# Attention's small work dealt out anew among ACT, DVE and POOL in a fused attention and mixture-of-experts kernel

## The chip, the cores and the metric

The kernel runs on one core of one Trainium2 chip. The metric is the device time of one execution in microseconds (us). The core has five engines with queues of their own, each of which works strictly in its queue's order: TensorE (PE in the profile, its weight loads PEld), VectorE (DVE), ScalarE (ACT), GpSimd (POOL) and SyncE (SP), which here only issues transfers. Engines wait for each other by semaphores.

## The reference

Sixteen batches of 128 tokens of width 512 go through two blocks, all in fp32:

```python
x = x + xattn(layernorm(x), ctx, ctx)     # 32 query heads, 8 key heads of width 16; keys = values = ctx
x = x + ffn(layernorm(x))                 # gate over 32 experts, top 8 in 4 of 8 groups, plus a shared expert

def layernorm(x, eps=1e-5):
    m = mean(x); v = var(x)
    return (x - m) / sqrt(v + eps)
```

In the attention each key head of 16 columns serves four query heads; scores are divided by 4 (the root of the head's width), go through a softmax and weight the values. In the second block each token's normalised row is multiplied with the gate's weights; the gate's best eight experts and the shared expert compute `(silu(x @ w1.T) * (x @ w3.T)) @ w2.T`, and the experts' results are added with the gate's weights.

## The kernel before

**The whole.** `attention_small()` (L271) computes both normalisations, the attention and the gate's logits. `experts()` (L1011) then routes the tokens (`route()`, L1088), computes the shared expert, gathers each expert's tokens from a table `rows` in memory (L1411), multiplies them with the expert's weights (L1483, L1537) and adds them to the output (L1509). The change touches attention alone.

**The order** of PE, DVE, ACT and POOL inside attention is the program's order, written out by hand (`manual_schedule`, L182). The tile framework adds the semaphore waits that the data and the buffers need. Instructions that read or write one and the same PSUM tile are kept in order as well.

**Steps.** An item is a batch b and a parity i: half of the key heads of that batch. There are 32 items, `items[n] = (n // 2, n % 2)`, and step n of the loop at L615 does, in this order:

1. the functions listed for the head of step n (`head`, L616);
2. `scores(n)` (L449): four row-packed matmuls into two PSUM tiles `sc` (two buffers in all), and on ACT two exps `p` of 128x1024 (L464);
3. `values(n - 1)` (L467): four matmuls into `oT` (one buffer), copied to `oTs` by DVE (L479);
4. in some steps `gate_parts` (L528: four matmuls and a copy on ACT, L540);
5. `transposes(*sets)` (L414): PE turns up to two sets of 128x512 into halves of one PSUM tile `x` (one buffer). The sets are `queries(n // 2 + 1)` (L439) in even steps, `added(n - 2)` (L499), and `turn_of(b)` (L506) from step 13 on, mostly in odd steps. When all are turned, each set's own function uses its half: for queries a copy to `qT` (L445, on DVE), for an attention output `add` (L485: on DVE the reciprocal `ri`, L488, and the product `at`, L490; on POOL the addition to `x`, L497), for a gate row a copy to `xnT` (L508, on ACT);
6. in some steps `gate_sums` (L542: two small matmuls and a copy to `logits` on DVE, L549);
7. the functions listed for the tail of step n (`tail`, L638).

**What the heads and tails hold** (L566 to L611):

- `layernorm_stats(b, mv)` (L89): on DVE `bn_stats` (L91) and `bn_aggr` (L92) of one batch. The first normalisation's run at steps 0 to 15, two in some of them. The second normalisation's need both halves of a batch added on POOL; batch b's stand at the tail of step 2b + 4, those of batch 13 at the head of step 30.
- `layernorm_rstd` (L94): 1/sqrt(v + eps) by a guess and three Newton rounds, 14 small instructions on POOL or 11 on DVE, for a group of batches at once. The first normalisation has groups of 1 and 3 on DVE and of 4, 4 and 4 on POOL (steps 3, 8 and 16), the second four groups of 3 and one of 2 on POOL (steps 9, 15, 21, 27 and 30) and one of 2 on DVE behind the loop.
- `rows_of(b)` (L390): on DVE the normalised queries `xq` of a batch.
- `keys(k)` (L342): for four batches at once, the transposed context times a mask of odd or even heads, two instructions of 128x512 into `kz`. The first quarter's are on ACT (L346), the other three quarters' on POOL (L348) at the heads of steps 4, 9 and 17. `values_of(k)` (L354) copies the values `va` of four batches: ACT for the first quarter, POOL for the others.
- `gate_rows(b)` (L215): the second normalisation's row `xn` (L217), on POOL for batches 0 to 11 and on DVE for 12 to 15, and one store of 256 KB to `rows` from SP (L220). Rows 9, 10 and 11 stand at the heads of steps 28, 29 and 30.
- `key_lengths(k)` (L364): ACT squares a quarter's context (L366), DVE sums it (L371), at steps 17 to 20; the longest is found at step 21.

**Before the loop** ACT holds, in this order, the two keys of the first quarter (L346) and `values_of(0)` (L355, which waits for the load of `cn`); DVE holds the first batch's statistic, its Newton rounds, its queries and the first copy to `qT`. **Behind the loop** (L643 to L683) come the last outputs, the last gate rows and their logits, with the first matmuls of the shared expert as filler; `both` (L656) is one PSUM tile whose halves take turned gate rows and the last output.

Of the kernel before, what the change touches and what calls it, by code (L numbers as in the profile page):

```python
# [9 lines left out]
F32 = mybir.dt.float32  # L10
# [36 lines left out]
def tile_xattn_moe(  # L47
# [40 lines left out]

    def layernorm_stats(b, mv):  # L89
        st = xnp.tile([P, 6], F32, tag="st", name="st")  # L90
        nc.vector.bn_stats(st, xs[b])  # L91
        nc.vector.bn_aggr(mv[:, b, :], st)  # L92

    def layernorm_rstd(mv, rstd, eng):  # L94

        n = mv.shape[1]
        ve = xnp.tile([P, B], F32, tag="ve", name="ve")[:, 0:n]
        eng.tensor_scalar(ve, mv[:, :, 1], EPS, None, ALU.add)
        r = xnp.tile([P, B], I32, tag="r", name="r")[:, 0:n]
        eng.tensor_scalar(  # L100
            r, ve.bitcast(I32), -0.5, float(0x5F3759DF), ALU.mult, ALU.add
        )
        r = r.bitcast(F32)
        h = xnp.tile([P, B], F32, tag="h", name="h")[:, 0:n]
        for i in range(3):
            to = rstd if i == 2 else r
            if eng is nc.vector:
                eng.scalar_tensor_tensor(h, r, -0.5, r, ALU.mult, ALU.mult)
                eng.tensor_tensor(h, h, ve, ALU.mult)
                eng.scalar_tensor_tensor(to, h, 1.5, r, ALU.add, ALU.mult)  # L110
            else:
                eng.tensor_tensor(h, r, r, ALU.mult)
                eng.tensor_tensor(h, h, ve, ALU.mult)
                eng.tensor_scalar(h, h, -0.5, 1.5, ALU.mult, ALU.add)
                eng.tensor_tensor(to, h, r, ALU.mult)

    def normalized_T(b, mv, rstd, dst, ps_tr):

        xn = xnp.tile([P, D], F32, tag="xn", name="xn")
        nc.vector.tensor_scalar(  # L120
            xn, xs[b], mv[:, b, 0:1], rstd[:, b : b + 1], ALU.subtract, ALU.mult
        )
        tr = ps_tr.tile([P, ND, P], F32, tag="tr", name="tr")
        for k in range(ND):
            nc.tensor.transpose(tr[:, k, :], xn[:, ts(k, P)], ident)
        nc.scalar.copy(dst, tr)
        return xn
# [4 lines left out]
    sap = ctx.enter_context(tc.tile_pool(name="sap", bufs=1))  # L132
    mv1 = const.tile([P, B, 2], F32, name="mv1")
    rstd1 = const.tile([P, B], F32, name="rstd1")
    mv2 = const.tile([P, B, 2], F32, name="mv2")
    rstd2 = const.tile([P, B], F32, name="rstd2")
    logits = const.tile([P, NT, E], F32, name="logits")
# [17 lines left out]
    more = const.tile([1, 1], I32, name="more")  # L155

    def first_rstd(first, n, eng=nc.vector):
        bs = slice(first, first + n)
        layernorm_rstd(mv1[:, bs, :], rstd1[:, bs], eng)

# [47 lines left out]

    def second_rstd(first, n, eng=nc.vector):
        bs = slice(first, first + n)  # L210
        layernorm_rstd(mv2[:, bs, :], rstd2[:, bs], eng)

    xn2 = {}

    def gate_rows(b, eng):  # L215
        xn = xnp.tile([P, D], F32, tag="xn", name="xn")
        eng.tensor_scalar(  # L217
            xn, xs[b], mv2[:, b, 0:1], rstd2[:, b : b + 1], ALU.subtract, ALU.mult
        )
        nc.sync.dma_start(rows[ts(b, P), 0:D], xn)  # L220
        xn2[b] = xn
# [49 lines left out]
    def attention_small():  # L271


        with ExitStack() as ph:
# [66 lines left out]

            def keys(k):  # L342
                for i in range(2):
                    to, of = kzs[k % 2][:, :, i, :], cTs[:, quarter[k], :]
                    if k == 0:
                        nc.scalar.activation(to, of, AF.Copy, scale=odd[:, i : i + 1])  # L346
                    else:
                        nc.gpsimd.tensor_scalar(to, of, odd[:, i : i + 1], None, ALU.mult)  # L348

# [40 lines left out]
            def rows_of(b):  # L390
                xqs[b] = ap2.tile([P, G, KV, HD], F32, tag="xq", name="xq")
                nc.vector.tensor_scalar(
                    xqs[b].rearrange("p g k d -> p k g d"),
                    xs[b].rearrange("p (k g d) -> p k g d", g=G, d=HD),
                    mv1[:, b, 0:1],
                    rstd1[:, b : b + 1],
                    ALU.subtract,
                    ALU.mult,
                )

            fixed_values(0, nc.vector)
            layernorm_stats(0, mv1)
            first_rstd(0, 1)
            rows_of(0)
            layernorm_stats(1, mv1)
            keys(0)
            values_of(0)

# [30 lines left out]
            def queries(b):  # L439

                xn = xqs.pop(b).rearrange("p g k d -> p g (k d)")

                def then(x):
                    qTs[b] = ap2.tile([P, 2, 2, P], F32, tag="qT", name="qT")
                    nc.vector.tensor_copy(qTs[b], x)  # L445

                return xn, False, then
# [111 lines left out]
            def at_head(n, f, *a):  # L559
                head.setdefault(n, []).append((f, a))  # L560

            def at_tail(n, f, *a):
                tail.setdefault(n, []).append((f, a))


            for b in (2, 3):  # L566
                at_head(0, layernorm_stats, b, mv1)
            at_tail(0, first_rstd, 1, 3)
            at_tail(0, rows_of, 1)
            at_tail(1, rows_of, 2)  # L570
            for b, n in ((4, 1), (5, 1), (6, 2), (7, 2)):
                at_tail(n, layernorm_stats, b, mv1)
            at_head(3, first_rstd, 4, 4, nc.gpsimd)
            for k in range(2, NTB):
                for m in range(4):
                    at_head(8 * k - 10 + m // 2, layernorm_stats, 4 * k + m, mv1)
                at_head(8 * k - 8, first_rstd, 4 * k, 4, nc.gpsimd)
            for b in range(3, B):
                at_head(2 * b - 3, rows_of, b)

            at_head(3, fixed_values, 1, nc.gpsimd)
            at_head(4, keys, 1)
            at_head(5, values_of, 1)
            for k in range(2, NTB):
                at_head(8 * k - 7, keys, k)
                at_head(8 * k - 6, values_of, k)
            for k in range(NTB):
                at_head(17 + k, key_lengths, k)
            at_head(21, longest)
            at_tail(21, longest_turned)  # L590
            at_tail(22, compare_lengths)


            turned, parts, sums = {}, {}, {}
            at_head(4, fold_of)
            for first in range(0, 12, 3):
                for b in range(first, first + 3):
                    at_tail(2 * b + 4, layernorm_stats, b, mv2)
                at_head(2 * first + 9, second_rstd, first, 3, nc.gpsimd)
            for b in range(11):  # L600
                n = min(2 * b + 13, b + 21)
                turned[n] = b
                at_head(max(n - 3, b + 19 if b > 8 else 0), gate_rows, b, nc.gpsimd)
            at_head(30, gate_rows, 11, nc.gpsimd)
            for b in range(0, 8, 2):
                parts[2 * b + 16], sums[2 * b + 17] = b, b
            parts[31] = 8
            at_tail(28, layernorm_stats, 12, mv2)
            at_head(30, layernorm_stats, 13, mv2)
            at_head(30, second_rstd, 12, 2, nc.gpsimd)  # L610
            at_tail(31, gate_rows, 12, nc.vector)  # L611

            transposes(queries(0))
            keep_warm(FILL[-1])
            for n in range(N):  # L615
# [8 lines left out]
                if n in parts:  # L624
                    gate_parts(parts[n])
                sets = []
                if n % 2 == 0 and 0 < n // 2 < B - 1:
                    sets.append(queries(n // 2 + 1))
                if n > 1:
                    sets.append(added(*items[n - 2]))  # L630
                if n in turned:
# [25 lines left out]
            tr, o = both[:, 0], both[:, 1]  # L657
            gate_turn(12, tr)
            last = oTs.pop(items[N - 1])
            for g in range(G):  # L660
                nc.tensor.transpose(o[:, g], last[:, g, :], ident)
            add(*items[N - 1], o.rearrange("p g (j e) -> p j g e", e=HP))
            gate_turn(13, tr)
            layernorm_stats(14, mv2)
            gate_parts(10)
            filler(1)
            gate_sums(10)
            nc.scalar.activation(table, table, AF.Sigmoid)
            layernorm_stats(15, mv2)
            second_rstd(14, 2)  # L670
            filler(1)
# [13 lines left out]
    def attention_general():  # L685
# [3 lines left out]
        with ExitStack() as ph:  # L689
# [24 lines left out]
            for b in range(B):  # L714
                layernorm_stats(b, mv1)
            first_rstd(0, B)

            qTs, vas, scs, pTs, os = {}, {}, {}, {}, {}

            def prepare(b):  # L720
# [9 lines left out]
                qT = ap2.tile([P, ND, P], F32, tag="qT", name="qT")  # L730
                normalized_T(b, mv1, rstd1, qT, ps_tr)
                qTs[b], vas[b] = qT, va
# [71 lines left out]
        with ExitStack() as ph:  # L804
            ps_lg = ph.enter_context(tc.tile_pool(name="ps_lg", bufs=1, space=PSUM))
            ps_tr = ph.enter_context(tc.tile_pool(name="ps_tr", bufs=1, space=PSUM))
            for b in range(B):
                layernorm_stats(b, mv2)
            second_rstd(0, B)
            for b in range(B):  # L810
# [860 lines left out]
```

## Time and profile before

| | us |
|---|---|
| median of 3 timed runs | 1009.43 (1009.0 to 1010.62) |
| the profiled execution | 1003.76 |
| its span, first to last instruction | 1002.0 |
| start of step 0's score matmuls | 9.19 |
| start of step 31's score matmuls | 117.96 |
| busy in the span: PE / POOL / DVE / ACT | 972.2 / 507.9 / 294.2 / 285.2 |

All views are of the one profiled execution, and its span is shorter than what a timed run takes. In lines of the timeline the first two numbers are the start and the length in us, then engine, line of the kernel, operation and tiles (`out<-in`); a bracket gives the idle time of the engine just before, and what ended it. In lines by group `xcount` is the number of instructions, and behind the bar stand busy us, mean ns of one, and the idle time before them. An engine that waits is named first in the view of waits, then whom it waited for.

### The profile page before, as it was taken

To read this page: it belongs to the slowest core of one execution; us is meant where nothing else is said; L and a number is where in the kernel's file an instruction comes from. 1 tells how busy PE (TensorE), PEld (TensorE's weight loads), DVE (VectorE), ACT (ScalarE), POOL (GpSimd) and SP (SyncE) were. 2 spreads that over 40 slices of the span, in tenths; PEclk is the share of its full clock that TensorE was granted. 3 is DMA by queue.
4 is the path that set the end of the run, shared out by engine and by line. 5 is a ranking of instruction groups with operands and counts; after the bars stand their busy time and mean duration, and the time that the engine had idled before them with its cause. 6 is when DMAs were issued, how large, how long until landed. Compare 5 with 4: busy or idle time off the path is not lost.

```text
span 1002.0 us, 13955 instructions
## 1 busy us (share of the span) xinstructions
PE 972.2 (97%) x4965; PEld 550.7 (55%) x4965; DVE 294.2 (29%) x983; ACT 285.2 (28%) x444; POOL 507.9 (51%) x659
## 2 busy tenths in 40 slices
PE   9889989999999999999999999999999999999996
PEld 5233444445666646666666666667654444444453
DVE  8676659882211112111112111111121111211100
ACT  5656631331222223222222222222222222221221
POOL 3778732564545436445545454555464444456443
PEclk9999989999999999999999999999999999999998
DMA  9001111415757658667767676777676677666543
GB/s 300 20 33 43 54 43 65 167 65 180 170 122 168 135 136 180 145 153 185 159 151 160 153 162 152 162 177 170 137 171 157 142 168 194 146 157 165 120 67 45
DMA packets 59869, 137.15 MB, mean 137 GB/s; under 512 B 12168, under 2 KB 16392, under 8 KB 59792
## 3 DMA queue, kind: packets, MB, share of 16 engines
q0 software_dynamic: 32032, 69.25, 36.4%
q1 hardware_dynamic: 27680, 66.81, 19.6%
q8 instruction: 41, 0.67, 0.3%
q14 instruction: 36, 0.29, 0.1%
q10 hardware_dynamic: 80, 0.13, 0.0%
HBM read 96.71 MB, written 46.73 MB: 143 GB/s over the span
## 4 chain that ended last, share of the span: by engine, by line
PE 79%; DVE 5%; POOL 5%; issue 5%; DMA 3%; ACT 1%; POOLq 0%; DVEq 0%; ACTq 0%
PE gu L1483 42%; PE y L1537 21%; PE gu L252 5%; PE trx L1435 4%; POOL out_dram L1509 3%; PE y L1330 2%; DMA out_dram<-yw,token 2%; PE sc L454 2%; PE oT L470 1%; DVE st L91 1%; PE x L427 1%; PE tok L997 1%; DVE oTs L479 1%; POOL kz L348 1%; DVE at L490 0%
## 5 line engine op out<-in xcount | busy, mean ns | idle before, releaser
L1483 PE MATMUL gu<-xnT,wup 128*128 128x256 f32 (+27 forms) x1664 | 490.6, 445 | 1.2 <-ACT xnT L1451 1.2
L1483 PEld LDWEIGHTS gu<-xnT,wup 128*128 128x128 f32 x1664 | 315.1, 190 | 193.0 <-issue 133.2
L1509 POOL DMA_INDIRECT out_dram<-yw,token x150 | 234.7, 1564 | 348.8 <-ACT yw L1546 238.5
L1537 PE MATMUL y<-wdn,sa 128*128 128x512 f32 (+2 forms) x672 | 263.4, 600 | 0.0
L1494 DVE TENSOR_TENSOR sa<-sl,gu 128x256 f32<-128x256 f32 (+27 forms) x104 | 52.2, 502 | 625.0 <-PE gu L1483 625.0
L1411 POOL DMA_INDIRECT xg<-rows,token x138 | 141.8, 1028 | 47.0 <-issue 26.3
L1546 ACT ACTIVATE yw<-y,wt 128x512 f32<-128x512 f32 x138 | 94.8, 687 | 244.0 <-PE y L1537 206.3
L1537 PEld LDWEIGHTS y<-wdn,sa 128*128 128x128 f32 (+2 forms) x672 | 98.3, 171 | 94.2 <-issue 84.8
L1492 ACT ACTIVATE sl<-gu 128x256 f32<-128x256 f32 (+27 forms) x104 | 46.6, 448 | 249.8 <-PE gu L1483 249.8
L464 ACT ACTIVATE p<-sc 128x1024 f32<-128x1024 f32 x64 | 62.2, 1024 | 26.7 <-PE sc L454 26.6
L1451 ACT COPY xnT<-trx 128x512 f32<-128x512 f32 x69 | 37.2, 589 | 91.5 <-PE trx L1435 91.5
L252 PE MATMUL gu<-xnT,sup 128*128 128x512 f32 x128 | 60.0, 608 | 0.7 <-ACT ssl L260 0.7
L991 POOL TENSOR_SCALAR hq<-slice_q,sq 128x138 f16<-128x138 f16 x32 | 34.7, 1098 | 35.2 <-DVE sq L1296 18.5
L454 PE MATMUL sc<-qT,kz 32*128 32x512 f32 x256 | 46.5, 642 | 0.5 <-ACT p L464 0.4
L1435 PEld LDWEIGHTS trx<-ident,xg 64*128 64x128 f32 x1104 | 37.2, 139 | 17.8 <-issue 17.5
L470 PE MATMUL oT<-p,va 128*32 128x512 f32 x256 | 35.8, 633 | 9.2 <-DVE oTs L479 9.2
L1435 PE MATMUL trx<-ident,xg 64*128 64x64 f32 x1104 | 42.1, 226 | 0.0
L1451 DVE COPY xnT<-trx 128x512 f32<-128x512 f32 x57 | 39.3, 689 | 5.8 <-PE trx L1435 5.1
L497 POOL TENSOR_TENSOR x<-x,at 128x256 f32<-128x256 f32 x32 | 23.5, 736 | 32.5 <-DVE at L490 32.5
L252 PEld LDWEIGHTS gu<-xnT,sup 128*128 128x128 f32 x128 | 23.1, 193 | 24.4 <-issue 21.9
L1466 DVE SCALAR_TENSOR_TENSOR own<-expert,owner,xg 128x32 f32<-128x32 f32 x138 | 31.3, 246 | 0.0
L1330 PE MATMUL y<-sdn,sa 128*128 128x512 f32 x64 | 29.3, 596 | 0.0
(187 smaller groups left out, 481.4 us busy)
## 6 DMA issues: line engine op xcount, KB each, us to landing
wup<-in_w_dram SPq DMA_DIRECT2D x64, 512.0 KB, 5.5
wdn<-in_w_dram SPq DMA_DIRECT2D x32, 512.0 KB, 5.2
rows<-xn SPq DMA_DIRECT2D x16, 256.0 KB, 2.0
out_dram<-x SPq DMA_DIRECT2D x16, 256.0 KB, 3.1
x<-in_x_dram SPq DMA_DIRECT2D x15, 256.0 KB, 6.3
out_dram<-yw,token POOLq DMA_INDIRECT x150, 5.0
xg<-rows,token POOLq DMA_INDIRECT x138, 4.4
cTs<-in_cT_dram SPq DMA_DIRECT2D x4, 256.0 KB, 5.6
```

Of the source, the lines that this page charges most:

```text
L252: nc.tensor.matmul(acc, lhsT=sup[:, w, d, ts(i, P)], rhs=xnT[k][:, d, :], start=(d == 0), stop=(d == ND - 1),)
L454: nc.tensor.matmul(scs[j // 2][:, j % 2], lhsT=kzs[b // 4 % 2][rows, b % 4, i, :], rhs=qT[rows], start=True, stop=True, tile_position=(j * ...
L464: nc.scalar.activation(p, sc, AF.Exp, scale=1.0 / HD**0.5)
L1330: nc.tensor.matmul(y, lhsT=acts[b // 4][:, i, ts(b % 4, P)], rhs=sdn[:, i, :], start=(i == 0), stop=(i == NI - 1),)
L1411: nc.gpsimd.indirect_dma_start(out=t, out_offset=None, in_=rows[:, :], in_offset=bass.IndirectOffsetOnAxis(ap=token[:, j : j + 1], axis=0) ...
L1435: nc.tensor.matmul(trs[s // 2][:, h, s % 2, d, :], lhsT=xg[j][rows_of_half, ts(d, P)], rhs=ident[rows_of_half, rows_of_half], start=True, ...
L1451: copy(xnT[n % NTB][:, :, col : col + P].rearrange("p d (h t) -> p h d t", h=2), tr)
L1483: nc.tensor.matmul(acc[:, 0:m], lhsT=wup[k % NW][:, w, d, ts(i, P)], rhs=xnT[n % NTB][:, d, 0:m], start=(d == 0), stop=(d == ND - 1),)
L1494: nc.vector.tensor_tensor(acts[n % NTB][:, i, 0:m], banks[2][:, 0:m], acc[:, 0:m], ALU.mult)
L1509: ins = nc.gpsimd.indirect_dma_start(out=flat, out_offset=bass.IndirectOffsetOnAxis(ap=token2[:, k - 1 : k] if a else token[0:b, j : j + 1 ...
L1537: nc.tensor.matmul(y[c0:c1, :], lhsT=acts[n % NTB][:, i, col : col + c1 - c0], rhs=wdn[pieces[n][0] % NW][:, i, :], start=(i == 0), stop=( ...
L1546: nc.scalar.activation(yws[j], y, AF.Copy, scale=wt[:, j : j + 1])
```

## The change

Nothing is computed otherwise; instructions change their engine, their place in the order or their grouping.

- The copy to `qT` goes from DVE to ACT.
- The keys of the last three quarters go from POOL to ACT, one instruction at the head of a step each: steps 4 and 5, 9 and 11, 17 and 19.
- The first normalisation's statistics of batches 8 to 15 stand alone at the heads of steps 5, 7, 8, 9, 11, 13, 14 and 15. That of the second normalisation for batch 13 goes to the tail of step 30.
- Both normalisations share one array of statistics `mv` and one of results `rstd`, in an order (`FIRST`, `SECOND`) that lets one group of Newton rounds serve both. POOL's groups are now 4 (step 3), 7 (9), 7 (15), 3 (21), 3 (27) and 2 (31).
- Gate rows 9, 10 and 11 are made by DVE, at the heads of steps 29, 30 and 31.
- Key lengths are taken at the heads of steps 8, 10, 12 and 14.
- In `transposes` the attention output comes ahead of the queries, in PE's order and in the order of the functions behind.
- Behind the loop, gate row 12 is turned after the last output is turned and added, no longer ahead of it.

```diff
-            def keys(k):
-                for i in range(2):
-                    to, of = kzs[k % 2][:, :, i, :], cTs[:, quarter[k], :]
-                    if k == 0:
-                        nc.scalar.activation(to, of, AF.Copy, scale=odd[:, i : i + 1])
-                    else:
-                        nc.gpsimd.tensor_scalar(to, of, odd[:, i : i + 1], None, ALU.mult)
+            def keys(k, i):
+                nc.scalar.activation(
+                    kzs[k % 2][:, :, i, :], cTs[:, quarter[k], :], AF.Copy, scale=odd[:, i : i + 1]
+                )
...
+    mv = const.tile([P, 2 * B, 2], F32, name="mv")
+    rstd = const.tile([P, 2 * B], F32, name="rstd")
+    FIRST = [*range(12), *range(15, 19)]
+    SECOND = [*range(12, 15), *range(19, 2 * B)]
...
+    def layernorm_rstd(first, n, eng=nc.vector):
...
+        eng.tensor_scalar(ve, mv[:, first : first + n, 1], EPS, None, ALU.add)
...
                 def then(x):
                     qTs[b] = ap2.tile([P, 2, 2, P], F32, tag="qT", name="qT")
-                    nc.vector.tensor_copy(qTs[b], x)
+                    nc.scalar.copy(qTs[b], x)
...
-            at_head(3, first_rstd, 4, 4, nc.gpsimd)
-            for k in range(2, NTB):
-                for m in range(4):
-                    at_head(8 * k - 10 + m // 2, layernorm_stats, 4 * k + m, mv1)
-                at_head(8 * k - 8, first_rstd, 4 * k, 4, nc.gpsimd)
+            at_head(3, layernorm_rstd, 4, 4, nc.gpsimd)
+            for b, n in zip(range(8, B), (5, 7, 8, 9, 11, 13, 14, 15)):
+                at_head(n, layernorm_stats, b, FIRST)
...
-            at_head(4, keys, 1)
+            at_head(4, keys, 1, 0)
+            at_head(5, keys, 1, 1)
             at_head(5, values_of, 1)
             for k in range(2, NTB):
-                at_head(8 * k - 7, keys, k)
+                for i in range(2):
+                    at_head(8 * k - 7 + 2 * i, keys, k, i)
                 at_head(8 * k - 6, values_of, k)
             for k in range(NTB):
-                at_head(17 + k, key_lengths, k)
+                at_head(8 + 2 * k, key_lengths, k)
...
-            for first in range(0, 12, 3):
-                for b in range(first, first + 3):
-                    at_tail(2 * b + 4, layernorm_stats, b, mv2)
-                at_head(2 * first + 9, second_rstd, first, 3, nc.gpsimd)
+            for b in range(14):
+                at_tail(2 * b + 4, layernorm_stats, b, SECOND)
+            for n, group in ((9, (8, 7)), (15, (15, 7)), (21, (22, 3)), (27, (25, 3)), (31, (28, 2))):
+                at_head(n, layernorm_rstd, *group, nc.gpsimd)
             for b in range(11):
                 n = min(2 * b + 13, b + 21)
                 turned[n] = b
-                at_head(max(n - 3, b + 19 if b > 8 else 0), gate_rows, b, nc.gpsimd)
-            at_head(30, gate_rows, 11, nc.gpsimd)
+                if b < 9:
+                    at_head(n - 3, gate_rows, b, nc.gpsimd)
+                else:
+                    at_head(n - 1, gate_rows, b, nc.vector)
+            at_head(31, gate_rows, 11, nc.vector)
...
                 sets = []
+                if n > 1:
+                    sets.append(added(*items[n - 2]))
                 if n % 2 == 0 and 0 < n // 2 < B - 1:
                     sets.append(queries(n // 2 + 1))
-                if n > 1:
-                    sets.append(added(*items[n - 2]))
...
-            gate_turn(12, tr)
             last = oTs.pop(items[N - 1])
             for g in range(G):
                 nc.tensor.transpose(o[:, g], last[:, g, :], ident)
             add(*items[N - 1], o.rearrange("p g (j e) -> p j g e", e=HP))
+            gate_turn(12, tr)
             gate_turn(13, tr)
```

## The prediction

> **What bounds the kernel now.** I read the busy time by stretches first. Step n is one item (a batch and half its key heads); its start is that of its first score matmul (L454): 9.19 for step 0, 14.80 (2), 46.60 (12), 55.66 (13), 89.80 (22), 117.96 (31). At 135.44 the tail has copied its second gate sum. Columns: length, then busy time of PE, PEld, DVE, ACT, POOL (instructions), granted clock, DMA.
>
> ```profile
> 14.80:55.66 40.86, 33.52 (x316) 12.37 (x312) 29.13 (x68) 21.32 (x22) 27.56 (x62) 0.96 0.32 112
> 55.66:89.80 34.14, 30.91 (x315) 12.45 (x313) 27.19 (x64) 22.14 (x29) 26.77 (x53) 1.00 0.11 40
> 89.80:117.96 28.16, 28.16 (x313) 12.06 (x313) 17.80 (x43) 19.96 (x25) 20.86 (x35) 1.00 0.11 40
> 135.44:1002.00 866.56, 852.58 (x3844) 497.62 (x3842) 201.40 (x749) 207.09 (x349) 420.23 (x460) 1.00 0.61 145
> ```
>
> The reader is to see two stretches of nine steps with the same matmuls (x315 and x313), one 6.0 us longer than the other. From 89.80 on PE is never idle; before it, PE waits. The last 866 us are PE's own and start when attention ends, so I carry a shift of attention to the end one to one. The view of waits for 9 to 121 us says who is late (total, times, longest):
>
> ```profile
> ACT p L464 <- PE sc L454: 26.6, 21, 7.2
> PEld oT L470 <- DVE oTs L479: 17.3, 10, 5.1
> ACT xnT L508 <- DVE at L490: 14.2, 9, 3.7
> DVE st L91 <- POOL x L497: 10.9, 4, 4.9
> ```
>
> PE waits for DVE, DVE for POOL. The timeline of POOL, DVE and PE around the longest wait:
>
> ```profile
> 42.09 0.73 POOL L497 TENSOR_TENSOR x<-x,at 128x256 f32<-128x256 f32 x1
> 42.80 3.11 POOL L348 TENSOR_SCALAR kz<-cTs,odd 128x512 f32<-128x512 f32 x2
> 46.00 0.24 POOL L98 TENSOR_SCALAR ve<-mv 128x3 f32<-128x3 f32 x1
> ...
> 49.63 0.19 POOL L115 TENSOR_TENSOR rstd<-h,r 128x3 f32<-128x3 f32 x1
> 49.79 0.72 POOL L497 TENSOR_TENSOR x<-x,at 128x256 f32<-128x256 f32 x1
> 50.54 0.69 DVE L91 BATCH_NORM_STATS2 st<-x 128x6 f32<-128x512 f32 x1 [4.90 <-POOL x L497]
> 52.75 1.94 PE L470 MATMUL oT<-p,va 128*32 128x512 f32 x8 [4.25 <-DVE oTs L479]
> ```
>
> POOL works in order: the add of item 7 (49.79) stands behind a Newton group (38.06 to 42.1), two key copies and a second group; the statistic waits for the add, the oTs copy for the statistic, the value matmuls for the copy. Step 12 takes 9.06 us. At 79.44 and 82.89 the same happens with less (steps 20 and 21: 5.42 and 4.83).
>
> **The change, part by part.** Durations are from these groups by form, and from the start's timeline:
>
> ```profile
> L217 POOL TENSOR_SCALAR xn<-x,mv,rstd 128x512 f32<-128x512 f32 x12 | 24.9, 2076 | 0.0
> L445 DVE COPY qT<-x 128x512 f32<-128x512 f32 x16 | 11.0, 687 | 2.4 <-PE x L427 2.4
> L348 POOL TENSOR_SCALAR kz<-cTs,odd 128x512 f32<-128x512 f32 x6 | 9.6, 1610 | 0.0
> L508 ACT COPY xnT<-x 128x512 f32<-128x512 f32 x12 | 7.0, 585 | 17.7 <-DVE at L490 16.4 <-PE sc L454 1.2
> L217 DVE TENSOR_SCALAR xn<-x,mv,rstd 128x512 f32<-128x512 f32 x4 | 2.5, 640 | 1.1 <-POOL rstd L115 1.1
> L346 ACT ACTIVATE kz<-cTs,odd 128x512 f32<-128x512 f32 x2 | 1.3, 714 | 4.0 <-DVE h L109 4.0
> ```
>
> *The start: +2.4.* The first qT copy goes to ACT, and there it is queued behind the values' copy, which waits for a load:
>
> ```profile
> 8.30 0.66 DVE L445 COPY qT<-x 128x512 f32<-128x512 f32 x1
> 9.19 1.14 PE L454 MATMUL sc<-qT,kz 32*128 32x512 f32 x8
> 9.67 0.62 ACT L355 COPY va<-cn 128x512 f32<-128x512 f32 x1 [1.50 <-DMA cn<-in_c_dram]
> ```
>
> So 9.67 + 0.62 + 0.585 + 0.2 to the matmul = 11.1 for step 0 in place of 9.19: 1.9 late. Step 2 waits for the second qT copy, behind the exps of step 1: 0.5 more, so it starts at 17.2. The 0.7 us that DVE gains does not help: it waits for the first value matmuls.
>
> *The steady step.* Two steps in the last stretch take 5.92 (2.71 + 3.22, steps 26 and 27), plus 0.99 where gate parts and sums fall (6.94 and 6.66). The exps start 1.23 us after the step, end at 3.18, and the next scores need their banks. Steps 9 and 10, without a gate row's turn, also sum to 5.92. So 2.96 per step is what PE and ACT allow as things stand.
>
> *Copies of queries on ACT.* In an even step oTs is copied until 2.8, the add's reciprocal and product end at 3.5. The built order lets the copy of qT wait for DVE from the third on: both read one PSUM tile. So it runs from 3.6 to 4.2; behind it in ACT's queue are the next exps, whose scores are ready at 2.71 + 1.23 = 3.94. They are 0.2 late, and the scores behind them too. Bounds: 0 (if the add is earlier) and 0.59 (nothing hidden) for each of the 14 copies of steps 2 to 28; I take 0.2, as ACT is idle for the rest of it now: +1.2 in steps 2 to 12, +0.8 in each later stretch.
>
> The Trainium skill, "ScalarE: Activation LUTs", Rules for kernel authors, speaks against this: add and multiply belong on VectorE rather than ScalarE, per element up to about three times faster in bf16. The rows here (fp32) have ACT at 585 and DVE at 687 ns; by the rule ACT's copy would be no cheaper than DVE's, and 14 copies exposed by 0.1 us more make it 1.4 us worse.
>
> *Keys on ACT.* Six copies at 714 ns for 1610 on POOL. At steps 5, 9, 11, 17, 19 each stands after a qT copy and ahead of exps: 0.71 less the slack of the following step, 0.6 each (bounds 0 and 0.71); at step 4 nothing precedes it: 0. So +1.9 before step 13, +1.2 after.
>
> *Key lengths* move from steps 17-20 to 8, 10, 12, 14: ACT has about 1 us idle there for 0.64; at 14 a turn copy takes it: +0.5. DVE's four reductions (0.68) fit where one statistic a step is left.
>
> *POOL* loses 6 x 1.61 = 9.7 of keys, two of eight Newton groups (14 instructions, 3.8 to 4.1 us each) = 7.8, and three gate rows = 6.2. A joint group is seven columns wide; two, three and four columns take 193, 199 and 218 ns in one line (L112), so at most some 0.3 us longer. In the new order the add of item 7 still stands behind one group. That group needs statistic 11, which DVE ends some 5.2 us after step 8 starts; group and add end at 9.9, and DVE reaches the statistic that wants them at 9.3: 0.6 late, within the slack of the next step. Two groups and two key copies no longer lie in a row, so the 6 us waits go. DVE is late next in steps 3 to 7 (statistics 4 to 7 are as before): 0.6.
>
> *Steps 2 to 12:* 11 x 2.96 = 32.6, + 1.2 + 1.9 + 0.6 = 36.3 for 40.86: **-4.6**. *Steps 13 to 21:* 28.16 + 0.8 + 1.2 + 0.5 = 30.7 for 34.14: **-3.5**. *Steps 22 to 30:* **+0.8**.
>
> *Late gate rows by DVE.* Rows 9 to 11 cost DVE 3 x 0.64. Their stores to rows go out one step later, in SP's same place; SP then waits for DVE; the first gather is at 227.7, so nothing waits. POOL's rows at 112.48, 115.24 and 118.00 no longer hold its adds: the exps of step 31 started at 120.73, 2.77 after it, where 1.25 is usual. *The tail's order:* transposing the last output ahead of row 12 takes a transpose (1.09) and a copy (0.58) out ahead of the last add, and puts them between it and the gate sum for whose copy DVE sat idle 3.56 us: 0, with 1.7 either way. Together **-1.2**.
>
> Sum: +2.4 - 4.6 - 3.5 + 0.8 - 1.2 = **-6.1**. The profiled execution took 1003.76 (span 1002.0 and 1.8 around it): 997.7. The three timed runs have median 1009.43, 5.7 above it; I see no reason in the page for the gap to move, so I forecast 1009.43 - 6.1 = **1003.3**.
>
> **Rivals.** *The clock.* After each long wait it is halved:
>
> ```profile
> 52.50:56.00 3.50, 3.25 (x28) 1.47 (x32) 1.71 (x5) 0.00 (x0) 3.50 (x4) 0.51 0.20 75
> 124.20:134.50 10.30, 8.68 (x40) 4.27 (x37) 4.18 (x10) 3.16 (x5) 2.79 (x4) 0.50 0.14 53
> ```
>
> The first dip is inside the 4.6 above (value matmuls 1.94 for 1.07). The second costs some 4 us on the tail's chain (L470 1.93 for 1.06, L252 1.87 for 1.1, and so on). If the shorter wait before step 31's values keeps the clock up, 3 more are gained: 1000.3. Against it: PE has only transposes for some 2.5 us there, where it had 2.8 (121.5 to 124.3). The Trainium skill, "TensorE: Matmul & The Clock Gate", Part 1: The HAM clock gate, says that a free-running window of 3413 ns decides; the dips here last 3.4 and 10.3 us, one window and three, and by the rule the phase of the window would decide between 1000.3 and 1003.3.
>
> *POOL stays late.* A joint group waits for a later statistic than either group did before, and an add stands behind it at steps 9 and 15. If each add is 1.5 us later than I have it, past the slack, 2 x 1.5 comes back: 1003.3 + 3.0 = 1006.3. For it: four such waits made the 10.9 us above. Against it: between the adds of items 6 and 7 POOL's queue falls from 7.0 us (42.8 to 49.8) to about 4.
>
> *Slower: ACT becomes the bound.* The exps wait for a qT copy, which waits for DVE's product. How dear this is shows at step 20: ACT's turn copy waited for a late product, and exps started at 83.91 for matmuls done at 80.69. If products end 0.7 us after where I put them (in before's even steps they end 1.5 us into the next step, after DVE's qT copy), each of 14 copies costs 0.87 in place of 0.2: +9.4, and 1012.7. It turns to a loss when a copy costs over 0.64 us (14 x 0.44 = 6.1). Against it: DVE drops the copy ahead of the product.
>
> *It cancels.* Copies cost about 0.6 each, the point just named: 1009.
>
> **How the numbers follow.** Forecast (1000.5 to 1006): 0.50. Clock up: 0.09. POOL late: 0.13. Cancels: 0.07. ACT the bound: 0.21. About 0.2%, 2 us, is what a measurement of this kernel can tell from none. Faster 0.72, same 0.07, slower 0.21. The range 998.0 to 1010.5 leaves out the worse half of the slower case and the best of the clock case. With all unknown costs at their upper ends it would be 14 x 0.39 + 5 x 0.11 + 1.7 = 7.7 more (1011.0), with all at their lower ends 14 x 0.2 + 5 x 0.6 + 1.7 = 7.5 less (995.8); all at once at one end is less likely than the two ends that I give.
>
> **What would show it.** Right: step 0 at 11.1; no statistic idle for POOL over 2 us; step 13 near 53.5, step 22 near 84, step 31 near 113; one halved clock, in the tail. Wrong: exps starting over 1.8 us after their step in most even steps (ACT bound); a long idle before L91 at steps 10 or 16 (POOL late). A different start of step 0 would show that the load or the order on ACT is not what I read.

## The result, and the profile after

The changed kernel takes 1001.83 us (median of 4 runs, 1000.62 to 1002.52) where the kernel before takes 1009.47 on the same chip (4 runs, 1009.0 to 1010.62): ratio 0.992, 95% interval 0.990 to 0.994, 7.6 us faster. The forecast was 6.1 us faster. The profiled execution of after took 1000.62, its span 998.8.

Line numbers of after differ: score matmuls L442, exps L452, value matmuls L458, copy to `oTs` L467, product L478, addition L485, copy of queries L433, keys L335, values L344, turned rows L496, gate sums' copy L537; a normalised row is L118 everywhere.

First the busy time by stretches, cut at the starts of steps 2, 13, 22 and 31 and at the sigmoid of the logits (columns as before: length, then PE, PEld, DVE, ACT, POOL with their instructions, granted clock, DMA):

```profile
16.39:51.95 35.56, 33.64 (x313) 11.96 (x313) 28.34 (x68) 27.45 (x34) 19.35 (x44) 1.00 0.30 106
51.95:82.96 31.01, 30.12 (x317) 12.42 (x314) 21.91 (x55) 24.39 (x33) 20.31 (x36) 1.00 0.12 43
82.96:111.21 28.25, 28.25 (x314) 12.45 (x313) 17.85 (x42) 22.12 (x29) 17.01 (x33) 1.00 0.13 48
111.21:136.31 25.10, 19.90 (x139) 10.06 (x136) 12.51 (x38) 8.50 (x15) 5.96 (x19) 0.86 0.15 54
```

The reader is to see that PE, idle for 7.3 of 40.86 us in the first of these stretches before, is now idle for 1.9 of 35.56; that POOL's busy time fell from 27.56 to 19.35 us there and ACT's rose from 21.32 to 27.45; and that the third stretch, where PE was never idle, is as long as it was. Against the terms on record:

| | before | after | change | on record |
|---|---|---|---|---|
| start of step 2 | 14.80 | 16.39 | +1.6 | +2.4 |
| steps 2 to 12 | 40.86 | 35.56 | -5.3 | -4.6 |
| steps 13 to 21 | 34.14 | 31.01 | -3.1 | -3.5 |
| steps 22 to 30 | 28.16 | 28.25 | +0.1 | +0.8 |
| step 31 to the logits' sigmoid | 26.05 | 25.10 | -0.95 | -1.2 |
| sum | | | -7.7 | -6.1 |

The sigmoid starts at 136.31 where it started at 144.01. Steps 13, 22 and 31 start at 51.95, 82.96 and 111.21 (on record: near 53.5, 84, 113). The waits from 9 to 121 us (who waits, for whom, total, times, longest):

```profile
DVE oTs L467 <- PE oT L458: 23.5, 17, 3.5
ACT qT L433 <- DVE at L478: 11.8, 12, 1.4
ACT xnT L496 <- DVE at L478: 8.1, 10, 2.6
ACT p L452 <- PE sc L442: 4.9, 8, 1.2
DVE st L91 <- POOL x L485: 1.4, 1, 1.4
```

The order has turned round: DVE waits for PE (23.5 us, before 11.9), ACT hardly waits for scores any more (4.9 for 26.6), and a statistic waits for POOL once, 1.4 us, in place of 10.9 us in four waits. The same place as in the timeline of before, now:

```profile
41.01 0.46 POOL L97 TENSOR_SCALAR ve<-mv 128x7 f32<-128x7 f32 x1 [0.89 <-DVE mv L92]
...
45.01 0.20 POOL L114 TENSOR_TENSOR rstd<-h,r 128x7 f32<-128x7 f32 x1
45.17 0.73 POOL L485 TENSOR_TENSOR x<-x,at 128x256 f32<-128x256 f32 x1
...
45.99 0.69 DVE L91 BATCH_NORM_STATS2 st<-x 128x6 f32<-128x512 f32 x1
46.25 0.64 PE L458 MATMUL oT<-p,va 128*32 128x512 f32 x4
```

The joint group takes 4.2 us (41.01 to 45.2) for seven columns; the add behind it ends at 45.9, and the statistic that wants it starts at 45.99 without any idle time in front.

### The profile page after: what moved, and what is told of

The parts are those of the page before. It is cut to its first block, busy times and chain, and to the rows that moved or that the text cites. A ratio compares the mean times of both kernels' runs of the same rounds, so it can differ in the third digit from the quotient of the medians.

```text
span 998.8 us, 13920 instructions
## 1 busy us (share of the span) xinstructions
PE 972.1 (97%) x4965; PEld 550.6 (55%) x4965; DVE 286.9 (29%) x970; ACT 296.6 (30%) x466; POOL 488.4 (49%) x622
## 4 chain that ended last, share of the span: by engine, by line
PE 88%; issue 3%; POOL 2%; ACT 2%; DMA 1%; DVE 1%; another core or an unknown queue 1%; SPq 0%; POOLq 0%; ACTq 0%; DVEq 0%
PE gu L1474 44%; PE y L1528 22%; PE gu L244 6%; PE sc L442 4%; PE trx L1426 4%; PE oT L458 2%; POOL out_dram L1500 2%; PE y L1321 1%; PE x L415 1%; DMA out_dram<-yw,token 1%; ACT p L452 1%; PE tok L988 1%; DMA cn<-in_c_dram 1%; PE lgT L519 0%
## 5 line engine op out<-in xcount | busy, mean ns | idle before, releaser
L452 ACT ACTIVATE p<-sc 128x1024 f32<-128x1024 f32 x64 | 62.2, 1026 | 5.1 <-PE sc L442 4.9
L442 PE MATMUL sc<-qT,kz 32*128 32x512 f32 x256 | 47.7, 640 | 4.1 <-ACT p L452 2.5
L485 POOL TENSOR_TENSOR x<-x,at 128x256 f32<-128x256 f32 x32 | 23.3, 730 | 43.8 <-DVE at L478 43.7
L458 PE MATMUL oT<-p,va 128*32 128x512 f32 x256 | 34.1, 605 | 0.0
```

What stands on the lines that cost most here:

```text
L442: nc.tensor.matmul(scs[j // 2][:, j % 2], lhsT=kzs[b // 4 % 2][rows, b % 4, i, :], rhs=qT[rows], start=True, stop=True, tile_position=(j * ...
L452: nc.scalar.activation(p, sc, AF.Exp, scale=1.0 / HD**0.5)
L458: nc.tensor.matmul(oT[j * HP : (j + 1) * HP], lhsT=vas[b // 4 % 2][:, b % 4, 2 * j + i, :], rhs=ps.pop((b, i, j)), start=True, stop=True, ...
```

## The experiments

Two theories. **A, POOL's queue:** the gain is that adds no longer stand behind Newton groups and key copies. **B, relief elsewhere:** DVE has lost the copies of queries and its paired statistics, and that is the gain. Chips differ by 5 to 6 us for one and the same kernel (the kernel before took 1004.21, 1009.26 and 1003.33 us on the chips of the three sets), so times are compared as ratios to the kernel before in the same set, and stretches of the profile among each other. The changed kernel itself was timed in the second set alone (experiment 9); for the other two its ratio there, 0.992, stands in. Its stretches are those of the table.

**1. The joint groups cut in two**

```diff
-for n, group in ((9, (8, 7)), (15, (15, 7)), ...
+for n, group in ((9, (8, 4)), (9, (12, 3)), (15, (15, 4)), (15, (19, 3)), ...
```

> The changed kernel with its two joint Newton groups of seven columns each cut into a group of four and one of three, at the same steps. Theory A: two more groups, 3.8 to 4.1 us each, ahead of the adds of steps 9 and 15; POOL's add is up to 4 us late there, the slack of a step is about 2, so 2 us are lost at each: 2 to 5 us slower than the changed kernel (1004 to 1007), with a wait of a statistic for POOL over 2 us. Rival B (DVE's and ACT's relief made the gain, POOL's groups are hidden): within 0.7 us of the changed kernel.

Measured: 0.997 of the kernel before (0.9955 to 0.9979), so most of the gain is gone. Steps 2 to 12 take 38.98 us (+3.4), steps 13 to 21 33.29 (+2.3). The timeline at the place of the last fence:

```profile
44.86 0.20 POOL L114 TENSOR_TENSOR rstd<-h,r 128x4 f32<-128x4 f32 x1
45.13 0.23 POOL L97 TENSOR_SCALAR ve<-mv 128x3 f32<-128x3 f32 x1
...
48.75 0.19 POOL L114 TENSOR_TENSOR rstd<-h,r 128x3 f32<-128x3 f32 x1
48.91 0.73 POOL L485 TENSOR_TENSOR x<-x,at 128x256 f32<-128x256 f32 x1
49.67 0.69 DVE L91 BATCH_NORM_STATS2 st<-x 128x6 f32<-128x512 f32 x1 [3.59 <-POOL x L485]
...
52.46 1.08 PE L458 MATMUL oT<-p,va 128*32 128x512 f32 x4 [2.08 <-DVE oTs L467]
```

Two groups take 7.9 us where one takes 4.2, the same add starts at 48.91 in place of 45.17, and the chain of before (add, statistic, oTs, value matmuls) is back with 3.59 us of idle DVE. The clock is halved once more behind it (50.5 to 57.4): PE is busy for 34.98 us with the matmuls that took 33.64, so by this measure at most 1.3 of the 3.4 us are the clock's. Theory A holds for the groups.

**2. The joint groups alone, on the kernel before.** Queries by DVE, keys on POOL, statistics in pairs, gate rows and tail are as before. The second normalisation's statistic of batch 13 and the last group of two stay where the change has them (tail of step 30, head of step 31).

> The kernel before with the joint Newton groups alone (statistics in pairs, keys on POOL, queries by DVE, key lengths, gate rows and tail as before). Theory A (the two groups less, at steps 9 and 15, are the gain): steps 2 to 12 shorten by 3 to 4 us and 13 to 21 by 2, 4 to 6 us faster than the kernel before (0.994 to 0.996). Rival (the groups count only because the other parts leave them no cover; in the kernel before, the key copies and the paired statistics keep POOL and DVE late anyway): under 2 us faster (over 0.998).

Measured: 1003.15 us against 1009.26, ratio 0.995 (0.9934 to 0.9964), where the whole change stands at 0.992 in the same set. Steps 2 to 12: 36.14 (before 40.86, whole change 35.56); steps 13 to 21: 32.58 (34.14 and 31.01). The grouping, with two instruction sequences less, makes 4.7 of the 5.3 us and 1.6 of the 3.1, without the 1.6 us that the change loses at the start. The rival falls.

**3. Keys back on POOL, at the new steps**

```diff
-nc.scalar.activation(kzs[...], cTs[...], AF.Copy, scale=odd[...])
+(k == 0: the same; else) nc.gpsimd.tensor_scalar(kzs[...], cTs[...], odd[...], None, ALU.mult)
```

> The changed kernel with the six later key copies back on POOL, at the same steps. Theory A (the relief of POOL's queue is what shortened steps 2 to 21): the copies (1.61 us each on POOL) stand ahead of POOL's adds again, statistics (L91) wait for POOL again by 1.5 us or more at steps 9 to 12 and 17 to 20, and although ACT is freed of 3.1 us by my terms, the kernel is 1 to 4 us slower than the changed one (1003 to 1006). Rival B (POOL has room enough now, ACT is what the steps wait for): steps 5, 9, 11, 17 and 19 shorten by 0.6 each and the kernel is about 3 us faster than the changed one (999).

Measured: 0.991 (0.9893 to 0.9926). Steps 2 to 12 take 34.69 (-0.9), steps 13 to 21 30.38 (-0.6). Neither theory had this right. Where ACT loses a key copy, the exps start 1.47 us after the step in place of 2.1, and steps 5, 9 and 11 shorten by 0.6 each, as on record. Step 20 is 0.7 shorter as well (3.38). A part is given back: step 6 is 0.9 longer, as its value matmuls now wait 0.85 us for DVE's `oTs` copy, and steps 12 and 14 are 0.3 and 0.5 longer; statistics wait for POOL 2.8 us in three waits, where it was 1.4 in one. By these stretches moving the keys to ACT cost 1.5 us net, half of my 3.1; the ratio is too coarse to tell it from the changed kernel's. It was not what freed POOL's adds. (Step 2 starts only at 17.55 here: the clock is halved from 10.8 to 14.2, in steps 0 and 1, which the edit doesn't touch.)

**4. Queries copied by DVE again, in the new order**

```diff
-nc.scalar.copy(qTs[b], x)
+nc.vector.tensor_copy(qTs[b], x)
```

> The changed kernel with the copies of the turned queries back on DVE, behind the add's product as the order now has it. My terms on record: the start comes back by 1.3 (measured 1.3 for step 0), 14 copies at 0.2 each give 2.8, so about 4 us faster than the changed kernel (998). Rival (it is DVE that had no room: 0.69 us more in each even step stands ahead of the next oTs copy, which the value matmuls wait for): 14 x 0.3 to 0.69 less 1.3, so 3 to 8 us slower (1005 to 1010).

Measured: 0.992 (0.990 to 0.9944), the changed kernel's own ratio. The start comes back (step 2 at 15.10 for 16.39), steps 2 to 12 take 37.00 (+1.4: step 6 alone takes 6.45 for 3.61, with a halved clock in it, and the others are 1.4 shorter together), steps 13 to 21 31.29 (+0.3), steps 22 to 30 28.16 (-0.1). So neither 14 x 0.2 nor 14 x 0.3 and more: on ACT the copy delays the exps of the next step by 0.24 us (they start 1.47 after it in place of 1.23), and that lies in slack.

**5. Statistics in pairs again** (steps 6, 6, 7, 7, 14, 14, 15, 15)

> The changed kernel with the first statistics of batches 8 to 15 in pairs at their old steps (6, 6, 7, 7, 14, 14, 15, 15). If one statistic a step matters (DVE is late where two of 0.9 us stand ahead of an oTs copy): steps 6, 7, 14, 15 are 0.5 to 0.9 longer each, 2 to 3 us slower than the changed kernel. If it only follows the joint groups: within 0.7 us.

Measured: 0.993 (0.9904 to 0.9948); steps 2 to 12 take 35.77 (+0.2), steps 13 to 21 30.97. With POOL on time it makes no difference how the first statistics are spread. With experiment 4, and with experiment 2, which has both of B's parts as before and still two thirds of the gain, theory B falls.

**6. Gate rows 9 to 11 back on POOL**

> The changed kernel with gate rows 9 to 11 back on POOL at their old steps (28, 29, 30). My term on record: with the tail's order -1.2, nearly all of it from the exps of step 31, so 1 us slower than the changed kernel, in the stretch from step 31 to the sigmoid. Rival: POOL has room at the end of attention now, 0.

Measured: 0.993 (0.9914 to 0.9943), the changed kernel in the same set 0.992. The starts of all steps agree with those of the changed kernel within 0.02 us once the start is aligned, and the exps of step 31 start 1.47 us after it in both. From step 31 to the sigmoid it takes 24.23 us, not longer but 0.9 shorter than in the changed kernel, with a clock that is halved for 3.4 us in place of 6.8. What I had put on these rows (2.77 in place of 1.25) was not theirs. Experiment 2 shows whose it was. It has the rows on POOL too, and POOL's add 0.68 us ahead of step 31, as in the kernel before; of what comes ahead of these exps only batch 13's statistic has moved, from the head of step 30 to its tail. Before, with step 31 at 117.96, and then experiment 2, with step 31 at 111.99:

```profile
117.28 0.74 POOL L497 TENSOR_TENSOR x<-x,at 128x256 f32<-128x256 f32 x1
118.05 0.69 DVE L91 BATCH_NORM_STATS2 st<-x 128x6 f32<-128x512 f32 x1 [2.40 <-POOL x L497]
120.25 0.58 ACT L508 COPY xnT<-x 128x512 f32<-128x512 f32 x1 [1.82 <-DVE at L490]
```

```profile
111.31 0.73 POOL L487 TENSOR_TENSOR x<-x,at 128x256 f32<-128x256 f32 x1
112.80 0.68 DVE L91 BATCH_NORM_STATS2 st<-x 128x6 f32<-128x512 f32 x1
112.97 0.59 ACT L498 COPY xnT<-x 128x512 f32<-128x512 f32 x1 [0.52 <-DVE at L480]
```

In the first the statistic keeps DVE waiting for 2.40 us ahead of the `oTs` copy and the product, and so holds ACT's copy and the exps behind it. In the second the product (112.46) comes first, and the exps start 1.47 us after the step.

**7. The tail's order undone** (row 12 turned ahead of the last output)

> The changed kernel with row 12 transposed ahead of the last output in the tail, as before. My term on record: 0, with 1.7 either way; the stretch from step 31 to the sigmoid takes 25.1 as in the changed kernel if the halved clock falls on it, 22.5 if it does not, and less than 0.7 beyond that is due to the order.

Measured: 0.994 (0.9922 to 0.9959); from step 31 to the sigmoid 25.17 us, with a halved clock from 121.1 to 127.9 as in the changed kernel (121.2 to 128.1). Zero, as on record.

**8. The kernel before once more**

> The kernel before once more, unaltered. The profiled execution of before stood 5.7 us under the median of its timed runs, that of the changed kernel 1.2. If the difference lies in the chip (the first experts' matmul 11.8 us behind token on one chip, 14.7 to 14.8 on another, whatever the kernel), this profile shows the distance of the other kernels of this set, 11.8 or 14.8, and its span lies within 1 us of its timed runs. Rival: the distance is a property of the kernel: 11.8 here while the kernels derived from the changed one show 14.8 in the same set.

Measured: 1003.65 us median of 10 runs against 1003.33 of the same kernel's other runs, ratio 1.001 (1.0002 to 1.0022), which shows how far to trust a tenth of a per cent. Its profile has the same stretches (40.86 and 34.22), but its tail keeps the full clock:

```profile
118.22:141.05 22.83, 17.73 (x138) 8.72 (x136) 12.43 (x37) 8.68 (x15) 8.01 (x21) 1.00 0.19 70
```

The same instructions take 22.83 us here and 26.05 in the first profile (there halved from 124.2 to 134.5): the clock of the tail comes and goes between executions of one kernel and is worth 3.2 us. This profiled execution (1001.11 us) is the fastest of the ten, 2.5 under their median and not within 1 us of it as expected. The distance from `token` to the experts' first matmul is 11.79 us, as in every kernel of this set.

**9. The changed kernel once more**

> The changed kernel once more, unaltered, on the chip of the other runs of this set, so that they can be compared with it there. If its 7.6 us are attention's: 0.990 to 0.994 of the kernel before. If the 2.9 us that its first profile shows between token and the first matmul of the experts (14.66 in place of 11.78) belong to the kernel, they come again; if they are chance, this distance is 11.8. The same for the halved clock in the tail (121.2 to 128.1): 31 to the sigmoid takes 25.1 with it and about 22.5 without.

Measured: 1000.51 us against 1009.26, ratio 0.992 (0.9911 to 0.9937). The stretches are those of after to 0.02 us, but for the start (step 0 at 9.85, not 10.49) and the tail (25.36). Distance from `token` to the experts' first matmul: 14.80 us, and 14.78 to 14.81 in the other three kernels of this set. ACT's copy of the first turned slice, in this profile and then in that of experiment 10:

```profile
232.65 1.07 ACT L1442 COPY xnT<-trx 128x512 f32<-128x512 f32 x2 [14.77 <-remote]
```

```profile
226.44 1.07 ACT L1442 COPY xnT<-trx 128x512 f32<-128x512 f32 x2 [11.76 <-PE trx L1426]
```

In the first the copy is released by an event that the profile can't name, 3.0 us after PE's transposes are recorded as done. All eight kernels of the other two sets show 11.78 or 11.79, among them kernels that differ from the changed one by a few lines of attention. So it goes with the chip of this set, not with the change; what it is, is open.

**10. The first values behind the first queries**

```diff
 for i in range(2):
     keys(0, i)
-values_of(0)
...
 transposes(queries(0))
+values_of(0)
```

> The changed kernel with the copy of the first quarter's values (which waits for the load of cn) moved behind the first copy of queries in ACT's order. If the start term is a wait in ACT's queue: step 0 starts at 9.2 to 9.4 in place of 10.49, and if the steps that follow keep the 1.3 us, the kernel is 1.3 us faster than the changed one (1000.5). Rival: step 2 waits for the values or for the batch's statistics anyway and the kernel gains under 0.5 us.

Measured: 0.990 (0.9887 to 0.992). The start in the changed kernel, and then in this one:

```profile
9.34 0.62 ACT L344 COPY va<-cn 128x512 f32<-128x512 f32 x1 [2.32 <-DMA cn<-in_c_dram]
9.86 0.58 ACT L433 COPY qT<-x 128x512 f32<-128x512 f32 x1
10.49 1.14 PE L442 MATMUL sc<-qT,kz 32*128 32x512 f32 x8 [1.24 <-ACT qT L433]
```

```profile
8.51 0.59 ACT L432 COPY qT<-x 128x512 f32<-128x512 f32 x1 [0.84 <-PE x L414]
9.22 0.62 ACT L344 COPY va<-cn 128x512 f32<-128x512 f32 x1
9.48 1.14 PE L441 MATMUL sc<-qT,kz 32*128 32x512 f32 x8
```

The copy of queries no longer stands behind a load that it does not need. Step 0 starts 1.0 us earlier, and the 1.0 is still there at step 31 (110.19 for 111.21): the start term is a wait in ACT's queue. The start varies between executions: 9.85 to 10.63 in the seven profiles with the changed order, 9.15 to 9.48 in the three with the values behind (this one and experiments 11 and 12). In this profile the tail keeps its clock as well and takes 22.53 us.

**11. Values behind, keys on POOL, the last value matmuls ahead of the transposes of item 30**

```diff
-transposes(added(*items[N - 2]), turn_of(11))
 values(*items[N - 1])
+filler(1)
+transposes(added(*items[N - 2]), turn_of(11))
...
     nc.tensor.transpose(o[:, g], last[:, g, :], ident)
+filler(1)
```

> The changed kernel with three edits: values of the first quarter copied behind the first queries, key copies of the later quarters on POOL again, and in the tail the last value matmuls ahead of the transposes of item 30, with two of the eight shared matmuls that fill gaps moved to the front of the tail. From the runs so far: start 1.0, keys 1.5, both in the steps; the tail's values start about 2 us earlier (at exps' end in place of behind a turn's copy), of which 1 may reach the end: 3.5 us faster than the changed kernel without the tail's halved clock in either. Rival: the start's gain and the keys' gain are the same slack of ACT and do not add: 2 us.

Measured: 998.51 us against 1009.26, ratio 0.990 (0.9886 to 0.9917); the changed kernel of this set 1000.51. Step 31 starts at 108.67 (after_again, the ninth, 110.56): start (0.7, as the ninth starts early) and keys (1.2) add, -1.9, where 2.5 was expected. The tail has a halved clock for 3.4 us (117.1 to 120.5) and takes 24.39. The last values start 3.5 us after step 31 and not 5.7, but that alone gains little: the whole is 2.0 us faster than the changed kernel by the medians, not 3.5.

**12. The same with the tail dealt out anew.** In the changed kernel the statistic of batch 15 stood on DVE behind the copy of a gate sum:

```profile
120.80 0.69 DVE L91 BATCH_NORM_STATS2 st<-x 128x6 f32<-128x512 f32 x1
127.36 0.22 DVE L537 COPY logits<-lg 128x64 f32<-128x64 f32 x1 [5.66 <-PE lg L534]
127.50 0.68 DVE L91 BATCH_NORM_STATS2 st<-x 128x6 f32<-128x512 f32 x1
```

```diff
 gate_turn(13, tr)
-layernorm_stats(14, SECOND)
+for b in (14, 15):
+    layernorm_stats(b, SECOND)
+layernorm_rstd(SECOND[14], 2)
+gate_rows(15, nc.vector)
+gate_rows(14, nc.vector)
 gate_parts(10)
 ...
```

ACT's table for the sigmoid is also loaded earlier, rows 15 and 14 are turned ahead of the gate sums of 12, and two more filler matmuls go to the front.

> The version with the early values copy, key copies on POOL and the early last value matmuls, with the tail dealt out anew: the statistic of batch 15 and the last Newton group no longer stand behind the copy of a gate sum on DVE (in the changed kernel the statistic waited from 121.7 to 127.50), the last rows are turned ahead of the gate sums of 12, and ACT's table is loaded ahead of the copies. The last logits then come 8 to 9 us after the last add's product in place of 15: 4 us faster than the version without it, 6 us faster than the changed kernel. Rival: the end of the tail is not on the path (the routing, or the shared part of the experts on PE, ends last): as fast as the version without it.

Measured: 989.79 us (989.52 to 990.04) against 1003.33, ratio 0.987 (0.9854 to 0.989), the fastest of all. DVE in its tail:

```profile
118.83 0.68 DVE L91 BATCH_NORM_STATS2 st<-x 128x6 f32<-128x512 f32 x1
119.75 0.69 DVE L91 BATCH_NORM_STATS2 st<-x 128x6 f32<-128x512 f32 x1
...
122.87 1.00 DVE L118 TENSOR_SCALAR xn<-x,mv,rstd 128x512 f32<-128x512 f32 x2
123.78 0.21 DVE L538 COPY logits<-lg 128x64 f32<-128x64 f32 x1
...
129.69 0.22 DVE L538 COPY logits<-lg 128x64 f32<-128x64 f32 x1 [2.15 <-PE lg L535]
```

The two statistics now follow each other, and the Newton rounds and both rows are done before the gate sum is copied. The last logits come 11.2 us after the last product (118.49), not 8 to 9; in experiment 10, whose tail has the full clock too, it is 13.0 (in the changed kernel 15.6, with its halved clock). From step 31 to the sigmoid it is 21.30 us, at the full clock: 1.2 less than the 22.53 of experiment 10 at the full clock, and 3.1 less than experiment 11 with its halved window. By the ratios it is 2.9 us ahead of experiment 11, where 4 was expected; by the stretches the tail's order makes 1.2 of it, and the clock a good part of the rest.

## Why the prediction was right, and where its steps were off

**What bounds it: right.** POOL's late adds made the waits, and their going made most of the gain. Experiment 2 gives the size: joint groups alone make two thirds of it (0.995 of 0.992), and without them (experiment 1) what is left is 0.997. The prediction gave the relief to three causes by POOL's busy time (9.7 us of keys, 7.8 of groups, 6.2 of rows). The runs show one: the group that stood directly ahead of an add. Keys (experiment 3) and rows (6) took time from POOL's total, and none to speak of from a wait.

**Start, +2.4: too dear by 0.8.** The mechanism is shown by experiment 10. The size hung on the landing of one load: the values' copy started at 9.34 for the 9.67 of before, the copies overlapped by 0.1, and the matmul followed 0.15 sooner than taken; the second copy, behind the exps of step 1, cost 0.3 and not 0.5. Step 0 started between 9.85 and 10.63 in the seven profiles with the same code there.

**Copies of queries, 0.2 each: the delay right, its price wrong.** Exps of odd steps are 0.24 late, and steps 22 to 30 are 0.09 us longer in all, not 0.8: the step after has the slack. The step that failed is that a delay of exps was charged to PE without the next step's slack taken off, which was done for the keys. The Trainium skill ("ScalarE: Activation LUTs", Rules for kernel authors) has add and multiply on VectorE rather than ScalarE, with a figure for bf16; its row does not name copies. For these fp32 copies the preference is not borne out: 586 ns on ACT against 687 on DVE, and the same ratio for the whole kernel in experiment 4.

**Keys on ACT, 0.6 each:** seen as such at steps 5, 9 and 11; net 1.5 of the 3.1 (of which +1.9 is really 3 x 0.6 = 1.8), since experiment 3 shows POOL's side of the trade.

**Steps 2 to 12 and 13 to 21:** -5.3 and -3.1 for -4.6 and -3.5. Without the 1.2 and 0.8 put on the copies of queries the sums would have been -5.8 and -4.3, so the other terms were too good by 0.5 and 1.2; as much as the latter stands at steps 20 and 21 (4.04 and 3.95 us, 1.2 more than steps 24 and 25 together); experiment 3 shows 0.7 of it to be the keys', the rest no experiment took apart. Of the 3.1, joint groups alone give 1.6; queries, statistics and rows moved back change little (experiments 4 to 6), and keys moved back gain. The parts that were not tried alone are the key lengths, which left steps 17 to 20, and the order of the transposes: the other 1.5 would be theirs, by exclusion only.

**Late gate rows, nearly all of -1.2: failed.** Experiment 6 has the same exps with the rows on POOL. The step that failed is that the rows' delay of POOL's adds was taken to reach the exps of step 31 of itself; it did so through batch 13's statistic at the head of step 30, and experiment 2 shows that with the statistic at the tail the exps start 1.47 us after the step although POOL's rows and adds stand as before. Nor did the 1.3 us by which they come sooner reach the end. At equal clock the tail gained 0.3 (22.83 to 22.53, experiments 8 and 10), the rest of 0.95 is the clock's (halved for 10.3 us before, for 6.9 after), so that -0.95 stands near -1.2 is luck. The tail's order was 0, as said.

**Profile and median.** The gap of 5.7 us was taken for a property of the kernel. By the runs it lies in the chip: the profile of before has 11.79 us between `token` and the experts, and the kernel before takes 1003 to 1004 us on the chips that show this, 1009 on the one that shows 14.8, with a halved clock behind it that cost 1.6 us in three profiles and 2.9 in two. The profile of before would then be from another chip than its timed runs; the record does not say which chips these were, so this part is inferred. The forecast survived, because only the difference of two kernels on one chip was carried over.

**Rivals.** *Clock up* did not happen in the profiled execution, and happened in those of experiments 1, 3, 8, 10 and 12. It differs between executions of one kernel (experiment 8), and was worth 2.6 us in after's tail (25.1 against 22.5). *POOL late* did not come: one wait of 1.4 us. *ACT the bound* did not come: exps started over 1.8 us behind their step only where a key copy stands (steps 5, 9, 11, 17, 19) and at step 14; in other even steps 1.2 to 1.5. *Cancels* did not come.

**The sum.** That it missed by only 1.5 us is in part luck: the copies of queries (by 2.7, if they cost as little everywhere as in steps 22 to 30) and the start (0.8) were too dear, the other terms of steps 2 to 21 (1.7) and the tail (0.25) too good, and these errors stand against each other.

## What to carry to other kernels

On an engine that works in order, ask what stands directly ahead of the one instruction that others wait for, not how busy the engine is: 3.7 us taken out at that place were worth more than 9.7 us of copies a step away. On POOL here many tiny instructions cost by their number, so two such chains over neighbouring columns are made one before anything is moved to another engine. And before profiles of two kernels are set against each other in absolute times, look for a stretch that both share and compare it first.

## What the runs showed of the hardware

- On POOL the Newton rounds cost nearly the same for seven columns as for three or four: 0.20 to 0.21 us busy and 0.29 from one to the next for 128x7, 0.19 to 0.20 and 0.28 for 128x3; a group of 14 takes 4.2, 4.1 and 3.8 us for seven, four and three.
- The halved clock of attention lasts 3.4, 6.8 to 6.9 or 10.3 us, and two executions of the kernel before have it for 10.3 us and not at all in tails that start at 117.96 and 118.22. The Trainium skill ("TensorE: Matmul & The Clock Gate", Part 1: The HAM clock gate) has a free-running window of 3413 ns; these lengths are one, two and three of it. The price of one such tail was 2.6 to 3.2 us, as large as a third of the change.
- One release on the way into the experts came 2.9 to 3.0 us later in the profiles of the changed kernel's result and of the four runs of the second set, where the kernel before takes 1009 us, and in none of the other nine; the profile names no cause.
